# A graph network's GRU aggregations: float32 operands, or bf16 parts that sum to them exactly

## Chip, core and metric

The kernel runs on one NeuronCore of one Trainium2 chip. The metric is the device time of one execution, in microseconds (us). The time before is a median of three runs. The profile is one further execution, recorded by the hardware profiler. Engines are named as in the profile: PE is TensorE, PEld its weight loads, DVE is VectorE, ACT is ScalarE, POOL is GpSimd, and SP is the queue that issues all the DMAs.

## What is computed

128 graphs of 128 nodes with 256 features each (`x` is 128 x 128 x 256, `adj` is 128 x 128 x 128 with integer entries). Two layers, both behind a layer norm and a ReLU and both added to the input:

```
h = relu(layernorm(x));  A = (adj != 0)
for l in 0, 1, 2:                              # gated graph layer
    m = h @ weight[l]
    aggr[t] = sum over s of A[s, t] * m[s]
    h = gru_cell(aggr, h, w_ih, w_hh, b_ih, b_hh)
x = x + h
h = relu(layernorm(x))                         # graph attention layer
Wh = h @ W.T;  e[i, j] = leaky_relu(Wh[i].a1 + Wh[j].a2), -inf where adj is 0
x = x + softmax(e) @ Wh
```

## The kernel before

**Tiling.** Four graphs form a group (G = 4, T = 512 nodes); 32 groups with three GRU layers each make 96 GRU steps. A group's state is kept in two layouts: `h`, rows of nodes (128 x 4 x 256, nodes on the partitions), and `hT`, columns (128 x 2 x 512, features on the partitions). The weight of the layer is folded into the input weights beforehand, so that a step needs first the sum over neighbours of the state itself: `gathered` (L630) takes, for each of two feature chunks and four graphs, one float32 matmul with a 128 x 128 piece of `h` as the stationary operand and the graph's A as the moving one (L637). Its two PSUM banks are copied by ACT into `aT` (L663), the columns of the aggregate. The same function serves the attention layer at the end, with softmax weights (tile e or prT) in A's place.

**One GRU step** (`gru_step`, L710) is two passes of `blocks` (L749) with seven `product`s each. They are Strassen-like block products: stationary sums of weight blocks, prepared once, against halves and sums of halves of hT and aT (`moving_sums`, L484, four subtractions on DVE for each, L493). All of them go into five PSUM banks: u, m (m7), c1 twice and c2. Between the products ACT copies u and m out (L757, L760, L770), and DVE adds u and m: into c2 at L763, into the SBUF tile c22 at L774. The next product into u needs those reads of u to be done. The gates follow on ACT (L795, L802, L830) and DVE (L837), then the new state on DVE: L682, L694, L696 and L698, each 128 x 1024 with operands in SBUF.

**From columns to rows.** After a step the new hT becomes h either by PE transposes (`rows`, L618, at the two ends of the run), or, for most steps, by DVE's 32 x 32 block transposes (L590) and two sets of four DMAs that pass through DRAM (`to_rows_by_blocks`, L581).

**The prologue and epilogue of a group.** `prologue` (L905) normalises x into h and makes A out of adj with `not_equal` (L919). `epilogue` (L940) is the attention layer; `mask` (L927) turns A in place into 0 and -1e30, which is added to the scores (L1055; for the two last groups by a matmul of ident with A, L1009). POOL does only three instructions of four columns for each layer norm (`norm_scales`, L454 to L458).

**What sets the order.** The program is one long list, written out by a planner that runs while the kernel is built (`Order`, L173). Each piece of work is a generator that yields an engine, a reckoned length, the time when its data are ready, and perhaps a `room`, a buffer that has to be free. The planner keeps a clock for each engine and takes the task that can start first, by rank. A clock "port" is shared by POOL and by those DVE operations that are yielded as DVE2: the planner never lets them overlap (L186, L196). The products of a GRU step are placed in a fixed order, with other DVE and ACT work filled in between (`fill`, L264) and other PE work between products (`matmuls`, L280). What comes out is the order of instructions on each engine; on the chip each engine runs its list in order, and an instruction starts as soon as its semaphores allow.

The steps of three groups take turns: (g, 0), (g-1, 1), (g-2, 2), and so on. `settle` (L1173) adds `inputs` (L647) of the next step's group while a step is being placed: the state's sums, the aggregation, the copies to aT and their sums.

Of the kernel before, what the change touches and what calls it, by code (L numbers as in the profile page):

```python
# [7 lines left out]

F32 = mybir.dt.float32
I32 = mybir.dt.int32  # L10
AF = mybir.ActivationFunctionType
ALU = mybir.AluOpType
AX = mybir.AxisListType

P = 128
D = 256
C = D // P
G = 4
T = G * P
H = T // 2  # L20
# [7 lines left out]
def preln_gnn_kernel(  # L28
# [14 lines left out]
    nc = tc.nc  # L43
# [4 lines left out]
    io = ctx.enter_context(tc.tile_pool(name="io", bufs=6))  # L48
# [8 lines left out]
    put = on_pe  # L57
# [4 lines left out]
    XT, AT = 3, 2  # L62
# [12 lines left out]
    work = ctx.enter_context(tc.tile_pool(name="work", bufs=2))  # L75
    gate = ctx.enter_context(tc.tile_pool(name="gate", bufs=2))
    small = ctx.enter_context(tc.tile_pool(name="small", bufs=4))

    ident = const.tile([P, P], F32, name="ident")
    make_identity(nc, ident)  # L80

    def borrowed(pool, shape, tag, name, columns, **bufs):
        tile_ = pool.tile(shape, F32, tag=tag, name=name, **bufs)
        flat = tile_.rearrange("p a b -> p (a b)") if len(shape) == 3 else tile_
        return flat[:, 0:columns]
# [10 lines left out]
            cols = slice(gates.start * D, gates.stop * D)  # L98
            dma(w[k][:, cols], weight[k * P : (k + 1) * P, cols])

    def load_weight(l, pool, shape, tag):
        w = borrowed(pool, shape, tag, f"wt_{l}", C * D)
        w = w.rearrange("p (c d) -> p c d", d=D)
        dma(w, weight_t[l].rearrange("(c p) d -> p c d", p=P))
        wt.append(w)
# [29 lines left out]

    zero = borrowed(gate, [P, C, T], "r", "zero", T, bufs=1).bitcast(mybir.dt.bfloat16)[:, 0:T]
    put(nc.vector.memset(zero, 0.0))
    c1 = [ps_sum.tile([P, 2, H], F32, name=f"c1_{n}") for n in range(2)]  # L140
    c2 = ps_sum.tile([P, 2, H], F32, name="c2")
# [23 lines left out]
    PE, ACT, DVE, DVE2, POOL, SP = "PE", "ACT", "DVE", "DVE2", "POOL", "SP"  # L165
    HOP = 0.2
# [6 lines left out]
    class Order:  # L173
        def __init__(self):
            self.free = dict.fromkeys((PE, ACT, DVE, POOL, SP, "port"), 0.0)
            self.tasks = []

            self.rooms = {room: [0.0] * 2 for room in ("tq", "x1", "prT", "e", "hs")}
            self.rooms |= {"misc": [0.0] * 3, "h": [0.0] * ROWS}
            self.next, self.room_of = dict.fromkeys(self.rooms, 0), {}  # L180

# [36 lines left out]
        def open(self, room, name):  # L218
            self.room_of[name] = room, self.next[room]
            self.next[room] = (self.next[room] + 1) % len(self.rooms[room])  # L220
            if room == "misc" and self.room_of[name][1] > 2:

                return more[self.room_of[name][1] - 3].rearrange("p n t -> p (n t)")
            if room == "misc":
                return ps_misc.tile([P, T], F32, tag="misc", name=name)
            if room == "h":
                return work.tile([P, G, D], F32, tag="h", name=name, bufs=ROWS)
            if room in ("prT", "e"):
                return work.tile([P, G, P], F32, tag=room, name=name)
            if room == "x1":  # L230
                return io.tile([P, G, D], F32, tag="x1", name=name, bufs=2)
            return work.tile([P, C, T], F32, tag=room, name=name)
# [79 lines left out]
    order = Order()  # L312
# [317 lines left out]
    def gathered(h, A, ready, name, graphs=range(G)):  # L630
# [13 lines left out]
            banks.append(pa)  # L644
        return banks, t

    def inputs(s, ready):  # L647

        name = f"{s.g}_{s.l}"
        s.tH, s.tA = {}, {}  # L650
        parts = len(s.parts())
        s.hidden = order.add(0, moving_sums(s.hT, s.tH, ready, f"h_{name}", parts))
        if s.l and not s.by_blocks():
            s.h, s.h_ready = yield from rows(s, ready, name)
        banks, ready = yield from gathered(s.h, s.A, s.h_ready, f"pa_{name}")
        order.close(f"h_{name}" if s.l else f"h_a{s.g}", ready)
        aT = None
        for c, pa in enumerate(banks):
            t = yield ACT, 0.57, ready
            order.close(f"pa_{name}_{c}", t)  # L660
            if aT is None:
                aT = columns_tile("aT", name)
            put(nc.scalar.copy(aT[:, c, :], pa))  # L663
        s.aT, s.aT_ready = aT, t
        yield from moving_sums(aT, s.tA, t, f"a_{name}", parts)

    def state_rows(s):
        s.h, s.h_ready = yield from to_rows_by_blocks(s.hT, s.hT_ready, f"{s.g}_{s.l}")
# [41 lines left out]
    def gru_step(s, last, part):  # L710
# [38 lines left out]
        def blocks(no, gates):  # L749

            m = gate.tile([P, 2, H], F32, tag="m", name=f"m_{name}_{no}")
            c22 = gate.tile([P, 2, H], F32, tag="c22", name=f"c22_{name}_{no}")
            done = product(gates, lambda q: u[:, q, 0:W], W11, (0, 0), None, banks["u"], True, (ACT,))
            t = order.take(ACT, bank_t, max(done, banks["c1_0"]))
            put(nc.scalar.copy(c1[0][:, :, 0:W], u[:, :, 0:W]))  # L757
            done = product(gates, lambda q: m7[:, q, 0:W], S3, None, T3, 0.0, True, (ACT,))
            tm = order.take(ACT, bank_t, done)
            put(nc.scalar.copy(m[:, :, 0:W], m7[:, :, 0:W]))  # L760
            done = product(gates, lambda q: u[:, q, 0:W], S2, None, T2, t, False, (DVE,))
            t = order.fixed(DVE, full_t, max(done, tm, banks["c2"]))
            put(nc.vector.tensor_tensor(  # L763
                c2[:, :, 0:W], u[:, :, 0:W], m[:, :, 0:W], ALU.add
            ))
            done = product(gates, lambda q: c1[0][:, q, 0:W], W12, (1, 0), None)
            yield done
            done = product(gates, lambda q: u[:, q, 0:W], S1, None, T1, t, False, (ACT,))
            t = order.take(ACT, bank_t, max(done, banks["c1_1"]))
            put(nc.scalar.copy(c1[1][:, :, 0:W], u[:, :, 0:W]))  # L770

            order.fill(t, (DVE,))
            tc22 = banks["u"] = order.fixed(DVE, full_t, t)
            put(nc.vector.tensor_tensor(  # L774
                c22[:, :, 0:W], u[:, :, 0:W], m[:, :, 0:W], ALU.add
            ))
            done = product(gates, lambda q: c2[:, q, 0:W], N22, None, T4, 0.0, False, (ACT, DVE))
            yield c22, tc22, done
            done = product(
                gates, lambda q: c1[1][:, q, 0:W], S4, (1, 1), None, t, False, (ACT, DVE)  # L780
            )
            yield done
# [26 lines left out]
        c22, t22, done = next(phase)  # L809
# [95 lines left out]
    def prologue(s):  # L905

        g = s.g
        kept = []
        parts = s.scales if g == 0 else [s.scales]
        for i, (rstd, nb, t) in enumerate(parts):  # L910
            n = G // len(parts)
            graphs = range(i * n, i * n + n)
            s.h, t = yield from norm_apply(s.xt, graphs, rstd, nb, t, f"a{g}", kept)
        s.h_ready = t
        if g + XT < NG:
            order.add(1, load_task(load_rows, xts, g + XT, t))
        t2 = yield DVE, 0.36, s.at_ready
        s.A = work.tile([P, G, P], F32, tag="A", name=f"A_{g}", bufs=6)
        put(nc.vector.tensor_scalar(s.A, s.at, 0.0, None, ALU.not_equal))  # L919
        if g + AT < NG:  # L920
            order.add(1, load_task(load_adjacency, ats, g + AT, t2))
        transposed = to_columns if g < 2 else to_columns_by_blocks
        s.hT, s.hT_ready = yield from transposed(s.h, t, f"a{g}")
        if s.entered:
            s.task = order.add(0, inputs(s, s.hT_ready))
# [14 lines left out]
    def epilogue(s, hT, graphs, ready):  # L940
# [46 lines left out]
        place = min(part.start, G - 2)  # L987
        for i in (1, 0):
            for k in graphs:
                first = not late and s.prT is None  # L990
                t = yield (DVE2, 0.53, ready, "prT") if first else (DVE2, 0.53, ready)
                if s.prT is None and late:
                    s.prT = io.tile([P, G, P], F32, tag="at", name=f"prT_{g}", bufs=AT)
                if s.prT is None:
                    s.prT = order.open("prT", f"prT_{g}")

                unused = s.prT[:, place : place + 2, :].rearrange("p k s -> p (k s)")
                put(nc.vector.scalar_tensor_tensor(
                    unused, h[:, k, :], rstd[:, k : k + 1] if final_one else 1.0, wa[:, i, :],
                    ALU.mult, ALU.mult,  # L1000
                    accum_out=(one, two)[i][:, k : k + 1],
                ))

        if late:
            t = yield PE, 4 * graph_t if end else graph_t, max(t, s.off_ready), "misc"
            p2 = order.open("misc", f"ps2_{name}")
            if end:

                put(nc.tensor.matmul(  # L1009
                    p2[:, cols], ident, s.A[:, part, :].rearrange("p k s -> p (k s)"),  # L1010
                    start=True, stop=False, skip_group_check=True,
                ))
            for k in graphs:
# [86 lines left out]
        final = graphs[-1] + 1 == G  # L1100
        if final:
            order.close(f"h_b{g}_0", ready)
        if final and not end:
            order.close(f"e_{g}", ready)
        for c, pq in enumerate(banks):
# [184 lines left out]
```

## Time and profile before

| | us |
|---|---|
| median of three runs (lowest, highest) | 2126.3 (2125.74, 2128.18) |
| profiled execution, first to last instruction (span) | 2124.5 |
| PE busy | 2116.6 |
| PEld busy | 1886.8 |
| DVE busy | 1733.1 |
| ACT busy | 1301.4 |
| POOL busy | 126.5 |

The page gives the span for the profiled execution and no other time of it; the median of the runs is 1.8 us above the span. The granted clock of TensorE is 1.000 on the mean. Busy times overlap, each engine has its own. In the groups, a line reads: line of the kernel, engine, operation, out<-in, shapes, count, then busy time in all, mean ns of one, and the idle time of that engine just before them with what ended it. The mean ns of a matmul is its latency, not its pace, because matmuls are pipelined; the pace is read from how far apart they start. In a timeline, a row is start, length, engine, line, operation and count.

### The profile page before, as it was taken

To read this page: it belongs to the slowest core of one execution; us is meant where nothing else is said; L and a number is where in the kernel's file an instruction comes from. 1 tells how busy PE (TensorE), PEld (TensorE's weight loads), DVE (VectorE), ACT (ScalarE), POOL (GpSimd) and SP (SyncE) were. 2 spreads that over 40 slices of the span, in tenths; PEclk is the share of its full clock that TensorE was granted. 3 is DMA by queue.
4 is the path that set the end of the run, shared out by engine and by line. 5 is a ranking of instruction groups with operands and counts; after the bars stand their busy time and mean duration, and the time that the engine had idled before them with its cause. 6 is when DMAs were issued, how large, how long until landed. Compare 5 with 4: busy or idle time off the path is not lost.

```text
span 2124.5 us, 32340 instructions
## 1 busy us (share of the span) xinstructions
PE 2116.6 (100%) x10865; PEld 1886.8 (89%) x10865; DVE 1733.1 (82%) x3771; ACT 1301.4 (61%) x2875; POOL 126.5 (6%) x200
## 2 busy tenths in 40 slices
PE   9999999999999999999999999999999999999999
PEld 7888888888888888888888888888888888888888
DVE  7778888888878888888888888888888888787777
ACT  5556666566656666666656666666666566665666
POOL 1000000000000000000000000000000000000000
PEclk9999999999999999999999999999999999999999
DMA  5334454554455444545344554445453544444311
GB/s 159 65 85 88 86 118 107 107 117 92 98 115 119 84 96 107 122 109 113 83 108 104 117 122 82 98 106 123 110 107 88 107 107 105 96 98 94 70 31 46
DMA packets 667975, 211.95 MB, mean 100 GB/s; under 512 B 578336, under 2 KB 644640, under 8 KB 667808
## 3 DMA queue, kind: packets, MB, share of 16 engines
q1 hardware_dynamic: 667808, 209.87, 44.3%
q8 instruction: 86, 1.41, 0.3%
q14 instruction: 81, 0.66, 0.1%
HBM read 121.91 MB, written 87.88 MB: 99 GB/s over the span
## 4 chain that ended last, share of the span: by engine, by line
PE 98%; DVE 1%; ACT 0%; DMA 0%; issue 0%; POOL 0%; SPq 0%; ACTq 0%; DVEq 0%
PE c L737 35%; PE u L737 35%; PE m L737 12%; PE pa L637 8%; PE po L1124 5%; PE pq L637 2%; PE pw L378 0%; DMA xt<-in_x 0%; PE c L1124 0%; PE u L1124 0%; ACT v L688 0%; PE c L637 0%; PE pr_o L527 0%; DVE st_a L440 0%; PE pr L527 0%; ACT e L1065 0%
## 5 line engine op out<-in xcount | busy, mean ns | idle before, releaser
L830 ACT ACTIVATE z<-c,brz 128x256 f32<-128x256 f32 (+1 forms) x388 | 186.2, 480 | 328.4 <-PE c L737 186.4
L737 PE MATMUL u<-t_h,s_hh 128*128 128x256 f32 (+1 forms) x1164 | 345.0, 378 | 0.9 <-DVE c L763 0.5
L737 PE MATMUL u<-t_a,s_f 128*128 128x256 f32 (+1 forms) x1164 | 312.3, 377 | 0.0
L737 PE MATMUL c<-aT,s_f 128*128 128x256 f32 (+1 forms) x1164 | 312.3, 377 | 0.0
L795 ACT ACTIVATE r<-c,brz 128x256 f32<-128x256 f32 (+1 forms) x388 | 175.3, 475 | 194.3 <-PE c L737 112.8
L763 DVE TENSOR_TENSOR c<-u,m 128x512 f32<-128x512 f32 (+1 forms) x194 | 134.6, 694 | 140.8 <-PE u L737 140.4
L737 PEld LDWEIGHTS u<-t_h,s_hh 128*128 128x128 f32 x1164 | 218.4, 190 | 31.3 <-ACT c L757 1.6
L737 PEld LDWEIGHTS c<-aT,s_f 128*128 128x128 f32 x1164 | 220.4, 190 | 28.9
L737 PEld LDWEIGHTS u<-t_a,s_f 128*128 128x128 f32 x1164 | 220.4, 190 | 29.0
L737 PE MATMUL c<-hT,s_hh 128*128 128x256 f32 (+1 forms) x780 | 229.8, 376 | 0.0
L837 DVE TENSOR_TENSOR v<-v,c 128x256 f32<-128x256 f32 (+1 forms) x388 | 153.6, 415 | 66.3 <-PE c L737 43.7
L770 ACT COPY c<-u 128x512 f32<-128x512 f32 (+1 forms) x194 | 109.7, 566 | 117.5 <-PE u L737 116.1
L760 ACT COPY m<-m 128x512 f32<-128x512 f32 (+1 forms) x194 | 112.7, 581 | 107.1 <-PE m L737 106.9
L802 ACT ACTIVATE v<-c,bhn 128x256 f32<-128x256 f32 (+1 forms) x388 | 173.0, 474 | 0.0
L737 PE MATMUL m<-t_h,s_hh 128*128 128x256 f32 (+1 forms) x582 | 172.3, 378 | 0.0
L737 PE MATMUL c<-t_h,s_hh 128*128 128x256 f32 (+1 forms) x582 | 172.1, 377 | 0.0
L737 PEld LDWEIGHTS c<-hT,s_hh 128*128 128x128 f32 x780 | 147.6, 190 | 19.2
L774 DVE TENSOR_TENSOR c<-u,m 128x512 f32<-128x512 f32 (+1 forms) x194 | 131.8, 679 | 37.9 <-ACT c L770 34.9
L737 PE MATMUL u<-aT,s_f 128*128 128x256 f32 (+1 forms) x582 | 156.2, 377 | 0.0
L737 PE MATMUL m<-t_a,s_f 128*128 128x256 f32 (+1 forms) x582 | 156.1, 377 | 0.0
L737 PE MATMUL c<-t_a,s_f 128*128 128x256 f32 (+1 forms) x582 | 156.1, 377 | 0.0
L757 ACT COPY c<-u 128x512 f32<-128x512 f32 (+1 forms) x194 | 109.8, 566 | 43.7 <-PE u L737 43.7
(164 smaller groups left out, 3928.4 us busy)
## 6 DMA issues: line engine op xcount, KB each, us to landing
z<-tq SPq DMA_DIRECT2D x248, 128.0 KB
h<-z SPq DMA_DIRECT2D x248, 128.0 KB
xt<-in_x SPq DMA_DIRECT2D x31, 512.0 KB
z_a<-tq_a SPq DMA_DIRECT2D x120, 128.0 KB
hT_a<-z_a SPq DMA_DIRECT2D x120, 128.0 KB
z_b<-tq_b SPq DMA_DIRECT2D x116, 128.0 KB
h_b<-z_b SPq DMA_DIRECT2D x116, 128.0 KB
x<-in_x SPq DMA_DIRECT2D x29, 512.0 KB
```

Source lines behind the costliest of these rows:

```text
L637: put(nc.tensor.matmul(pa[:, k * P : (k + 1) * P], h[:, k, c * P : (c + 1) * P], A[:, k, :], start=True, stop=True,))
L737: put(nc.tensor.matmul(to(q), S[0][:, gate_no, weight, :], moving, start=first and q == 0 and i == 0, stop=(i == len(ends) - 1), skip_grou ...
L757: put(nc.scalar.copy(c1[0][:, :, 0:W], u[:, :, 0:W]))
L760: put(nc.scalar.copy(m[:, :, 0:W], m7[:, :, 0:W]))
L763: put(nc.vector.tensor_tensor(c2[:, :, 0:W], u[:, :, 0:W], m[:, :, 0:W], ALU.add))
L770: put(nc.scalar.copy(c1[1][:, :, 0:W], u[:, :, 0:W]))
L774: put(nc.vector.tensor_tensor(c22[:, :, 0:W], u[:, :, 0:W], m[:, :, 0:W], ALU.add))
L795: put(nc.scalar.activation(r[:, o, cols], src, AF.Tanh, bias=brz[:, o : o + 1], scale=0.5))
L802: put(nc.scalar.activation(v[:, o, cols], src, AF.Identity, bias=bhn[:, o : o + 1], scale=0.5))
L830: put(nc.scalar.activation(z[:, o, cols], src, AF.Tanh, bias=brz[:, C + o : C + o + 1], scale=0.5))
L837: put(nc.vector.tensor_tensor(v[:, o, cols], v[:, o, cols], src, ALU.add))
L1124: put(nc.tensor.matmul(po[:, j, :], hs[:, c, k * P : (k + 1) * P], gwt[:, c, :], start=(c == 0), stop=(c == C - 1),))
```

## The change

The aggregations of the GRU steps no longer multiply float32 by float32. A becomes a bf16 tile (its entries are 0 and 1). h is split into three bf16 parts which sum to it exactly: the first is the upper half of each float32 word, read where it stands; POOL subtracts it from h (the remainder goes to a new tile `rest`); the second part is the upper half of each word of that remainder; POOL subtracts it too and writes the third part, in bf16, into the lower halves of the same words. Each aggregation matmul becomes three bf16 matmuls that accumulate in PSUM. The two subtractions stand in the planner's list ahead of the aggregation. The attention layer's own aggregation stays as it was.

To go with that: the matmul of ident with A (L1009) takes a bf16 view of ident; c22 gets one buffer where it had two; the buffers for the late prT are booked with the planner in a room of their own; `load_weight` passes buffer counts on.

```diff
+    ident_b = ident.bitcast(BF16).rearrange("p (c n) -> p c n", n=2)[:, :, 1]
...
+    def by_parts(tile_):
+
+        halves = tile_.bitcast(BF16).rearrange("p g (d n) -> p g d n", n=2)
+        return halves[:, :, :, 0], halves[:, :, :, 1]
+
+    def split(h, ready, name):
+
+        _, first = by_parts(h)
+        t = yield POOL, 2.4, ready, "rest"
+        rest = order.open("rest", f"rest_{name}")
+        third, second = by_parts(rest)
+        put(nc.gpsimd.tensor_tensor(rest, h, first, ALU.subtract))
+        t = yield POOL, 2.4, t - HOP
+        put(nc.gpsimd.tensor_tensor(third, rest, second, ALU.subtract))
+        return (first, second, third), t
+
+    def gathered_by_parts(parts, A, ready, name):
+
+        banks = []
+        t = yield PE, 0.17 * C * G, ready, "misc", C
+        for c in range(C):
+            pa = order.open("misc", f"{name}_{c}")
+            for k in range(G):
+                for i, h in enumerate(parts):
+                    put(nc.tensor.matmul(
+                        pa[:, k * P : (k + 1) * P],
+                        h[:, k, c * P : (c + 1) * P],
+                        A[:, k, :],
+                        start=(i == 0),
+                        stop=(i == len(parts) - 1),
+                    ))
+            banks.append(pa)
+        return banks, t
+
     def inputs(s, ready):
...
-        banks, ready = yield from gathered(s.h, s.A, s.h_ready, f"pa_{name}")
+        parts, ready = yield from split(s.h, s.h_ready, name)
+        banks, ready = yield from gathered_by_parts(parts, s.A, ready, f"pa_{name}")
         order.close(f"h_{name}" if s.l else f"h_a{s.g}", ready)
+        order.close(f"rest_{name}", ready)
...
-            c22 = gate.tile([P, 2, H], F32, tag="c22", name=f"c22_{name}_{no}")
+            c22 = gate.tile([P, 2, H], F32, tag="c22", name=f"c22_{name}_{no}", bufs=1)
...
-        s.A = work.tile([P, G, P], F32, tag="A", name=f"A_{g}", bufs=6)
+        s.A = work.tile([P, G, P], BF16, tag="A", name=f"A_{g}", bufs=6)
...
-                    p2[:, cols], ident, s.A[:, part, :].rearrange("p k s -> p (k s)"),
+                    p2[:, cols], ident_b, s.A[:, part, :].rearrange("p k s -> p (k s)"),
...
+        if final and late:
+            order.close(f"prT_{g}", ready)
```

More of the change, by code (lines that the diff above doesn't have):

```diff
@@ L10 @@
 I32 = mybir.dt.int32
+BF16 = mybir.dt.bfloat16
 AF = mybir.ActivationFunctionType
@@ L99, in load_gates, with load_weight @@
             dma(w[k][:, cols], weight[k * P : (k + 1) * P, cols])
-    def load_weight(l, pool, shape, tag):
-        w = borrowed(pool, shape, tag, f"wt_{l}", C * D)
+    def load_weight(l, pool, shape, tag, **bufs):
+        w = borrowed(pool, shape, tag, f"wt_{l}", C * D, **bufs)
         w = w.rearrange("p (c d) -> p c d", d=D)
@@ L133, in preln_gnn_kernel @@
         xts[g] = load_rows(g), 18.0 + 2.0 * g
-    zero = borrowed(gate, [P, C, T], "r", "zero", T, bufs=1).bitcast(mybir.dt.bfloat16)[:, 0:T]
+    zero = borrowed(gate, [P, C, T], "r", "zero", T, bufs=1).bitcast(BF16)[:, 0:T]
     put(nc.vector.memset(zero, 0.0))
@@ L176, in __init__ @@
             self.tasks = []
-            self.rooms = {room: [0.0] * 2 for room in ("tq", "x1", "prT", "e", "hs")}
+            self.rooms = {room: [0.0] * 2 for room in ("tq", "x1", "prT", "e", "hs", "rest", "late")}
             self.rooms |= {"misc": [0.0] * 3, "h": [0.0] * ROWS}
@@ L227, in open @@
                 return work.tile([P, G, D], F32, tag="h", name=name, bufs=ROWS)
+            if room == "late":
+                return io.tile([P, G, P], F32, tag="at", name=name, bufs=AT)
+            if room == "rest":
+                return work.tile([P, G, D], F32, tag="rest", name=name)
             if room in ("prT", "e"):
@@ L650, in inputs @@
         s.tH, s.tA = {}, {}
-        parts = len(s.parts())
-        s.hidden = order.add(0, moving_sums(s.hT, s.tH, ready, f"h_{name}", parts))
+        n_parts = len(s.parts())
+        s.hidden = order.add(0, moving_sums(s.hT, s.tH, ready, f"h_{name}", n_parts))
         if s.l and not s.by_blocks():
             s.h, s.h_ready = yield from rows(s, ready, name)
-        banks, ready = yield from gathered(s.h, s.A, s.h_ready, f"pa_{name}")
+        parts, ready = yield from split(s.h, s.h_ready, name)
+        banks, ready = yield from gathered_by_parts(parts, s.A, ready, f"pa_{name}")
         order.close(f"h_{name}" if s.l else f"h_a{s.g}", ready)
+        order.close(f"rest_{name}", ready)
         aT = None
@@ L664, in inputs @@
         s.aT, s.aT_ready = aT, t
-        yield from moving_sums(aT, s.tA, t, f"a_{name}", parts)
+        yield from moving_sums(aT, s.tA, t, f"a_{name}", n_parts)
     def state_rows(s):
@@ L989, in epilogue @@
             for k in graphs:
[L990 to L993, printed above, removed]
+                room = "late" if late else "prT"
+                t = yield (DVE2, 0.53, ready, room) if s.prT is None else (DVE2, 0.53, ready)
                 if s.prT is None:
-                    s.prT = order.open("prT", f"prT_{g}")
+                    s.prT = order.open(room, f"prT_{g}")
                 unused = s.prT[:, place : place + 2, :].rearrange("p k s -> p (k s)")
```

## The prediction

> **What bounds the kernel now.** I read the page's busy times first, then its chain, and then asked which engine is idle and how close the others follow.
>
> ```profile
> PE 2116.6 (100%) x10865; PEld 1886.8 (89%) x10865; DVE 1733.1 (82%) x3771; ACT 1301.4 (61%) x2875; POOL 126.5 (6%) x200
> ...
> PE 98%; DVE 1%; ACT 0%; DMA 0%; issue 0%; POOL 0%; SPq 0%; ACTq 0%; DVEq 0%
> PE c L737 35%; PE u L737 35%; PE m L737 12%; PE pa L637 8%; PE po L1124 5%; PE pq L637 2%; PE pw L378 0%; DMA xt<-in_x 0%; PE c L1124 0%; PE u L1124 0%; ACT v L688 0%; PE c L637 0%; PE pr_o L527 0%; DVE st_a L440 0%; PE pr L527 0%; ACT e L1065 0%
> ```
>
> TensorE (PE) is the bound: it carries 98% of the chain, and every nanosecond taken from its stream comes off the span, as long as nobody is late for it. The aggregations (pa, L637) are 8% of the chain. The second thing to see is VectorE (DVE) at 82%: it is not on the chain, but it is the engine that must never be late. The groups by form, then a timeline of 4 us in mid-run, show what it does and with how little room:
>
> ```profile
> L763 DVE TENSOR_TENSOR c<-u,m 128x512 f32<-128x512 f32 x190 | 132.9, 699 | 138.3 <-PE u L737 137.9
> ...
> L637 PE MATMUL pa<-A,h 128*128 128x128 f32 x1024 | 124.7, 275 | 0.0
> ...
> L637 PE MATMUL pa<-A,h_a 128*128 128x128 f32 x512 | 62.4, 275 | 0.0
> ```
>
> ```profile
> 1003.41 0.70 DVE L763 TENSOR_TENSOR c<-u,m 128x512 f32<-128x512 f32 x1 [0.49 <-PE u L737]
> ...
> 1004.23 0.41 PEld L737 LDWEIGHTS u<-t_h,s_hh 128*128 128x128 f32 x2
> ...
> 1004.44 0.59 PE L737 MATMUL u<-t_h,s_hh 128*128 128x256 f32 x2
> ```
>
> L763 reads bank u; the next matmul into u waits for it. It ends at 1004.11 and that matmul starts at 1004.44: 0.33 us of slack. In front of it DVE sat idle for 0.73 us on the mean (the page's 140.8 us over 194). So, twice in each GRU step, a DVE that is more than about 0.73 + 0.33 = 1.06 us behind stops TensorE.
>
> **Part 1, the matmuls: 96 aggregations change.** A float32 matmul leaves two passes in the trace: 1024 + 512 = 1536 passes over 96 aggregations is 16 each, for 8 matmuls. The timeline has such a set as x16 in 1.95 us; less the last one's 0.275 that is 1.675/15 = 0.112 us a pass, 16 x 0.112 = 1.79 us. After the change there are 24 bf16 passes. What is one worth? The trace has three bf16 matmuls, in the first microseconds:
>
> ```profile
> 1.17 1.46 PE L146 MATMUL c<-zero 128*128 128x512 bf16 x3 [1.17 <-DVE zero L139]
> ...
> 9.18 0.19 PEld L378 LDWEIGHTS pw<-wih,wt 128*128 128x128 f32 x1 [0.24 <-issue]
> ...
> 9.61 0.19 PEld L378 LDWEIGHTS pw<-wih,wt 128*128 128x128 f32 x1 [0.24 <-ACT h_a L471]
> ```
>
> Each of the three lasted about 0.635 (the median of that line), so they start (1.46 - 0.635)/2 = 0.41 us apart for 512 columns. In the same early stage float32 passes of 256 columns follow each other in 0.43 us (the loads at 9.18 and 9.61), against 0.216 later in the run. So a bf16 column costs half of a column of a float32 pass, and 128 of them 0.112/2 = 0.056 us. The weight load could bind instead. A float32 load of 128 columns paces its matmuls at about 0.10 to 0.11 us even when they stream only 2 columns (L409: eight pairs, first starts 50.4 to 51.1). A bf16 load was recorded at 105, 117 and 152 ns (L146), the float32 one at 190: 38 to 85 ns less, so a pace of 0.025 to 0.07 us. But those weights lay side by side; the new ones sit in every second 16-bit word, which no row shows. Bounds for the pass: 0.056 to 0.112 us. I take 0.056, since the bf16 rows are the nearer ones. **Gain: 96 x (1.79 - 24 x 0.056) = 96 x 0.446 = 42.8 us**; with 0.112 instead it is a loss of 96 x (2.69 - 1.79) = 86 us.
>
> The page "TensorE: Matmul & The Clock Gate" of the Trainium skill, section "Back-to-back issue gap", speaks against this: it gives about 81 ns for a sustained load-and-matmul pair at 128 columns. By that figure the sum below would have, as an estimate, a loss of 96 x (24 x 0.081 - 1.79) = 15 us where I have the gain of 42.8. No row here shows such a stream in bf16.
>
> The two end groups' matmul with ident (L1009, float32: 0.93 us for 512 columns, two halves of 0.43) goes to a quarter: about -1.3 us, at the very end.
>
> **Part 2, two GpSimd (POOL) instructions for each aggregation, 192 in all.** Each subtracts over 128x1024. POOL has no such row. Lower bound: DVE's own two-input operation of this size, 1.22 us (L694). Nearest POOL row: the 128x128 select of the identity took 0.293 us (masks.py:199), one input; eight times that is 2.3. The code reckons 2.4. I take 2.3 and keep 1.2 to 3. As work on POOL this is 192 x 2.3 = 442 us in an engine idle for 94% of the time, and in mid-run the transfers that bring the state's rows (h<-z on SP) are issued some 20 us ahead of their aggregation (the last at 769.4, the aggregation at 789.5), so TensorE should not wait for the parts themselves. Only at the start there is no such lead: h_a is done at 11.58, the first aggregation starts at 12.62 and its result is first used at 16.64. Two subtractions put it at about 16.4, and its use some 3 us later: **+3 us**.
>
> **What the POOL work meets is DVE.** The timeline around a small POOL chain shows it:
>
> ```profile
> 791.54 1.23 DVE L694 TENSOR_TENSOR hT<-hT,v 128x1024 f32<-128x1024 f32 x1 [0.37 <-ACT v L688]
> ...
> 792.27 0.59 POOL L456 TENSOR_SCALAR norm_b<-mv_b 128x4 f32<-128x4 f32 x1
> ...
> 792.80 1.23 DVE L696 SCALAR_TENSOR_TENSOR hT<-z,hT 128x1024 f32<-128x1024 f32 x1
> 792.94 1.15 POOL L458 TENSOR_TENSOR norm_b<-norm_b 128x4 f32<-128x4 f32 x1
> ```
>
> L458 works on 4 elements and takes 0.22 us elsewhere (its norm_a rows); here it takes 1.15 and ends 0.06 us after L696, a DVE operation with two inputs in SBUF. L456 likewise ends just after L694. So the two engines exclude each other for such operations; that a long POOL operation stops DVE in turn is my inference, since the trace has no long one. The page "SBUF — State Buffer" of the Trainium skill, section "Who interferes with whom", says so outright: whoever starts first holds the port for the whole instruction, and the other stands. If that rule held only in the direction that the rows show, the sum below would lose its stall term and end at 2085.
>
> How much does DVE lose? In 65 us (three GRU steps; window 765 to 830) its operations with two SBUF inputs (L493, L682, L694, L696, L698, L971, L998, L1055) take 30.5 us by their groups, the others 23.5, and 11.0 are idle. POOL gets six of the 2.3 us operations in there. During 2.3 us DVE has on the mean 30.5/65 x 2.3 = 1.1 us of work that cannot run; since its queue is in order, the first such operation holds up everything behind it, up to the full 2.3. Half of these operations follow one another without a gap, so I take 1.3: 6 x 1.3 = 7.8 us of delay per 65 us. Bounds: 0 (order perfect) to 6 x 2.3 = 13.8.
>
> What of that reaches TensorE? L763 comes six times in the 65 us, and each can swallow 1.06 us. Spread evenly, 1.3 on each, 0.24 x 6 = 1.4 us get through, or 1.4 x 32 = 46 us over the run. But the two subtractions are issued as a pair, and where both delays fall before the same L763, 2.6 us meet 1.06 and (2.6 - 1.06) x 3 x 32 = 148 us get through. The list that places instructions does know that DVE and POOL exclude each other and will move DVE's work around. Yet POOL's instruction waits only for its data, which are early, so it starts before the time that the list gave it and meets other DVE work. I take the middle: **+97 us** of waits of TensorE for DVE.
>
> The other edits cost nothing that I can find. c22 with one buffer: L774 writes it every 9 us or so, its readers (L795, L802, L830, L837) are done within about 4; were that cover gone, L774 would wait up to 0.5 us. A in bf16: L919, L930 and L1055 (0.42, 0.42, 0.69 us, 30-odd times) stay or shrink. The bookkeeping of the late prT buffer issues nothing new. A, written by DVE once a group, keeps its queue position, and SP's queue is not touched.
>
> **Sum**: 2124.5 (span) - 42.8 - 1.3 + 3 + 97 = 2180.4. The median of the runs shown is 2126.3, 1.8 above the profiled span; the page has no other time for that execution. So 2182.
>
> **Rivals.**
> - *Faster: the list's new order keeps two-input DVE work out of POOL's way.* One mechanism, at L763: it decides when the delay that passes the 1.06 us is under 41.1/192 = 0.21 us per subtraction. DVE's 11 us of idle in 65 exceed my 7.8 of delay, which speaks for it; POOL's early start speaks against. Stalls of 0 to 37 us give 2085 to 2122; at 10, 2095. Chance 0.33.
> - *The weight loads of strided bf16 run at float32 pace* (0.112 us): 2182 + 42.8 + 86 = 2311 with the stalls, 2214 without. Then the change doesn't do what it says, three passes are simply more than two. Chance 0.08.
> - *Gain and stall cancel*, within 0.2% (4.3 us, about what a measurement of this kernel can tell from no change): 0.05.
> - Forecast, stalls above the gain: 0.54, from 2131 to 2250.
>
> Faster 0.33, same 0.05, slower 0.62. Range: the low end is the rival with no stall, 2085, less 2 for a pass of 0.055; the high end is the lumped stall, 2182 + 51 = 2233, plus 17 for a subtraction of 2.5 us and more. That is 2083 to 2250; what is left out are the slow loads with stalls and a subtraction near 3 us. The likeliest case alone spans 2131 to 2250.
>
> **What would show it.** Aggregations: 24 passes in about 1.5 us, starts 56 ns apart (112: the loads bind). POOL near 570 us busy, subtractions of 2.3 us (more where they stand behind DVE). DVE: idle time before L493, L682, L694 to L698 or L998 put down to POOL; if there is none, my inference on the exclusion is wrong. PE: idle before u (L737) put down to DVE L763 or L774, in sum about 97 us, and PE's share of the chain below 95%. A wait of PE pa for POOL of more than a few us would mean that the parts come too late, which I have not priced.

## The result, and the profile after

| | before | after |
|---|---|---|
| median of the runs, us | 2126.3 | 2455.2 (2451.9 to 2459.4) |
| ratio to before, 95% interval | | 1.1545 (1.1529 to 1.1562) |
| span of the profiled execution, us | 2124.5 | 2453.0 |
| mean granted clock of PE | 1.000 | 0.948 |

The change costs 329 us. The prediction had the sign, with 2182, but the time lies 205 us above the top of its range. The page of after, its busy times, the clock in 40 slices, and the chain:

```profile
PE 2169.8 (88%) x11629; PEld 1880.9 (77%) x11630; DVE 1924.3 (78%) x3771; ACT 1304.8 (53%) x2875; POOL 510.9 (21%) x392
...
PEclk9999998999989989998999899989989998999998
...
PE 71%; DVE 20%; ACT 3%; issue 2%; DMA 2%; SPq 2%; POOL 0%; DVEq 0%; ACTq 0%
```

PE is now idle for 283 us of its span (2453.0 - 2169.8); before it was 8. DVE carries 20% of the chain where it had 1%. DVE issues the same 3771 instructions as before, but they are busy for 191 us longer. And the clock, which was 1.000, dips at regular places. The waits show whom PE waits for (columns: us in total, times, longest):

```profile
PE pq L643 <- DMA e<-z_e: 102.7, 8, 14.2
...
PE u L779 <- ACT c L799: 66.7, 10, 16.6
...
PE u L779 <- DVE c L805: 63.0, 24, 5.8
...
PE u L779 <- DVE c L816: 27.3, 18, 2.2
```

Two kinds stand out. The DVE rows are what the prediction had in mind: 63.0 + 27.3 = 90.3 us, many and short. The upper two are something else: eight waits of some 13 us in which the attention layer's scores product (pq, the old L637) waits for a DMA of softmax weights, and ten, of 6.7 us on the mean and 16.6 at most, before a product into u. Before, the first of these rows is absent and the second comes to 0.4 us, and in mid-run the change leaves the attention layer's work as it was.

The changed work itself is quick. Three rows in mid-run and a group by form:

```profile
1067.73 0.22 PE L677 MATMUL pa<-A,h 128*128 128x128 bf16 x1
...
1067.79 0.28 PE L677 MATMUL pa<-A,rest 128*128 128x128 bf16 x2
...
1067.90 0.22 PE L677 MATMUL pa<-A,h 128*128 128x128 bf16 x1
```

From the first of these passes to the fourth it is 0.17 us (1067.73 to 1067.90); over all aggregations a pass starts 56 ns after the one before it, in the median. The subtractions took 1.96 us in the median (1.89 to 2.87).

### The profile page after: what moved, and what is told of

It is laid out like the page before. It is cut to its first block, busy times and chain, and to the rows that moved or that the text cites. A ratio compares the mean times of both kernels' runs of the same rounds, so it can differ in the third digit from the quotient of the medians.

```text
span 2453.0 us, 34120 instructions
## 1 busy us (share of the span) xinstructions
PE 2169.8 (88%) x11629; PEld 1880.9 (77%) x11630; DVE 1924.3 (78%) x3771; ACT 1304.8 (53%) x2875; POOL 510.9 (21%) x392
## 4 chain that ended last, share of the span: by engine, by line
PE 71%; DVE 20%; ACT 3%; issue 2%; DMA 2%; SPq 2%; POOL 0%; DVEq 0%; ACTq 0%
PE u L779 27%; PE c L779 25%; PE m L779 8%; PE pa L677 4%; PE po L1166 4%; DVE prT L1038 3%; DVE t_a L499 3%; DVE hT L736 2%; DVE hT L738 2%; DVE hT L740 2%; SPq L61 2%; PE pq L643 1%; DVE c L805 1%; DVE t_h L499 1%; DMA e<-line 1%
## 5 line engine op out<-in xcount | busy, mean ns | idle before, releaser
L779 PE MATMUL u<-t_h,s_hh 128*128 128x256 f32 (+1 forms) x1164 | 366.1, 397 | 130.2 <-ACT c L799 66.7
L779 PE MATMUL u<-t_a,s_f 128*128 128x256 f32 (+1 forms) x1164 | 325.2, 390 | 0.0
L805 DVE TENSOR_TENSOR c<-u,m 128x512 f32<-128x512 f32 (+1 forms) x194 | 134.2, 692 | 155.9 <-PE u L779 135.1
L779 PEld LDWEIGHTS u<-t_a,s_f 128*128 128x128 f32 x1164 | 227.9, 197 | 32.8
L664 POOL TENSOR_TENSOR rest<-h 128x1024 f32<-128x1024 f32 x64 | 126.5, 1976 | 569.8 <-DMA h<-z 443.1
L812 ACT COPY c<-u 128x512 f32<-128x512 f32 (+1 forms) x194 | 109.7, 566 | 215.2 <-PE u L779 213.9
L460 POOL TENSOR_TENSOR norm_a<-norm_a,mhalf 128x4 f32<-128x4 f32 (+1 forms) x33 | 34.5, 1046 | 901.4 <-DVE norm_a L452 674.0
L666 POOL TENSOR_TENSOR rest<-rest 128x1024 bf16<-128x1024 f32 x96 | 209.3, 2181 | 7.5
L879 DVE TENSOR_TENSOR v<-v,c 128x256 f32<-128x256 f32 (+1 forms) x388 | 164.9, 447 | 56.8 <-PE c L779 44.0
L724 DVE SCALAR_TENSOR_TENSOR v<-r,v 128x1024 f32<-128x1024 f32 (+1 forms) x97 | 142.9, 1473 | 46.4 <-ACT v L844 45.7
L816 DVE TENSOR_TENSOR c<-u,m 128x512 f32<-128x512 f32 (+1 forms) x194 | 132.1, 681 | 55.6 <-ACT c L812 54.2
L779 PE MATMUL c<-t_a,s_f 128*128 128x256 f32 (+1 forms) x582 | 161.6, 388 | 0.0
```

The source lines that it names most:

```text
L664: put(nc.gpsimd.tensor_tensor(rest, h, first, ALU.subtract))
L666: put(nc.gpsimd.tensor_tensor(third, rest, second, ALU.subtract))
L724: put(nc.vector.scalar_tensor_tensor(v_, flat(r, cols), 1.0, v_, ALU.add, ALU.mult))
L779: put(nc.tensor.matmul(to(q), S[0][:, gate_no, weight, :], moving, start=first and q == 0 and i == 0, stop=(i == len(ends) - 1), skip_grou ...
L805: put(nc.vector.tensor_tensor(c2[:, :, 0:W], u[:, :, 0:W], m[:, :, 0:W], ALU.add))
L816: put(nc.vector.tensor_tensor(c22[:, :, 0:W], u[:, :, 0:W], m[:, :, 0:W], ALU.add))
```

## Experiments

A measure that I use below: for each matmul, the time from its start to the next one's, less the median of that interval for its kind. Summed over the run this is the time that PE lost to waits and to a lowered clock ("lost" from here on). The sum of the medians is its paced work. (A kind is a line of the kernel with its shapes.) Before: 2112.0 paced, 7.9 lost. After: 2067.4 and 380.9. So the matmul stream got 44.6 us shorter, and 373 us of loss came in. Theories for that loss: **LOCK** (the expectations call it PORT), a POOL subtraction stops DVE's two-input operations, and the late DVE stops PE; **ORDER**, the planner, which has to keep 4.8 us of the shared port free for each aggregation, writes a worse list; **EARLY**, POOL runs ahead of its place in the list, so that it meets DVE work which the list had kept clear of it.

**The matmuls alone** (`e1_no_remainders`)

```diff
-        parts, ready = yield from split(s.h, s.h_ready, name)
+        parts, ready = 3 * (by_parts(s.h)[1],), s.h_ready
```

> No POOL subtractions and none in the planner's list: the first bf16 part is multiplied three times, so the remainders are left out of the sum, and the 24 bf16 passes stay. Both theories: the matmuls alone, 2126 - 43 = about 2085, between 2075 and 2100. Above 2126 the loss would lie in the bf16 passes themselves, which neither theory holds.

Measured: 2096.9, ratio 0.986 (0.9845 to 0.9875), clock 0.999. Paced work is 2068.6, as in after. The net gain is 29.4 and not 43, because 21.5 us are lost instead of 7.9; the biggest piece is one wait of 5 us near the end of the run, which before does not have. The cause of the 373 us is thus not in the matmuls.

**The order alone** (`e2_plan_only`): everything is booked as in after, but the two POOL instructions are not issued. DVE's and ACT's instructions stand in the same order in both traces.

```diff
-        rest = order.open("rest", f"rest_{name}")
-        third, second = by_parts(rest)
-        put(nc.gpsimd.tensor_tensor(rest, h, first, ALU.subtract))
+        order.room_of[f"rest_{name}"] = "rest", order.next["rest"]
+        order.next["rest"] = (order.next["rest"] + 1) % 2
         t = yield POOL, 2.4, t - HOP
-        put(nc.gpsimd.tensor_tensor(third, rest, second, ALU.subtract))
-        return (first, second, third), t
+        return (first, first, first), t
```

> The order of all instructions as in the changed kernel (the planner still books 2 x 2.4 us of POOL and of the shared port for each aggregation), but the two subtractions are not issued; the first part is multiplied three times, so the remainders are left out. Theory PORT (long POOL instructions stop DVE, and TensorE waits for DVE): near the run without any remainders, 2085 to 2130. Theory ORDER (the planner, made short of port time, writes an order in which every third group's attention layer comes late and TensorE has to wait for its transfers): the loss stays, 2330 to 2455.

Measured: 2319.0, ratio 1.0908 (1.089 to 1.0926), clock 0.958. That is 222 us above e1, with no subtraction on POOL at all, and 11 us below what was expected of ORDER. Its page and its waits:

```profile
PE 2123.3 (92%) x11630; PEld 1867.4 (81%) x11630; DVE 1726.8 (75%) x3771; ACT 1310.8 (57%) x2875; POOL 109.1 (5%) x200
```

```profile
PE pq L643 <- DMA e<-z_e: 102.6, 8, 14.6
...
PE u L777 <- ACT c L797: 65.2, 10, 17.3
```

The long waits of after are all here (102.6 of 102.7 us, 65.2 of 66.7), while the DVE rows are nearly gone (1.6 us for L803, 0.9 for L814). So the long waits are ORDER, and the short ones for DVE are not. A timeline shows how such a wait is made:

```profile
616.52 1.03 PE L777 MATMUL c<-aT,s_f 128*128 128x256 f32 x4
...
617.58 0.42 DVE L877 TENSOR_TENSOR v<-v,c 128x256 f32<-128x256 f32 x1 [0.35 <-PE c L777]
...
617.92 0.70 DVE L616 STREAM_TRANSPOSE prT<-e 128x512 f32<-128x512 f32 x1
...
621.80 1.29 SPq L61 DMA_DIRECT2D z_e<-prT  x2
...
628.20 1.70 SPq L61 DMA_DIRECT2D e<-z_e  x4
...
631.63 3.75 PE L643 MATMUL pq<-e,h_b 128*128 128x128 f32 x16 [14.09 <-DMA e<-z_e]
```

Read it backwards. pq is next in PE's list; it needs e, which comes back from DRAM by the DMAs of 628.20; these need z_e; that needs DVE's transposition L616 at 617.92; and L616 stands in DVE's list behind L877, which waits for the product at 616.52 that PE has only just done. Nothing in this row of work can start before PE is through, and pq stands next in PE's list. Before, the same L610 runs at 778.16 and pq at 792.57, with the DMAs between them under PE's other work.

The long wait before u follows some 20 us later and is the same lump one step on. In after, for the pq wait at 897.6, the chain reads:

```profile
922.47 1.65 ACT e L1105 x8
924.11 0.95 ACT hs L1158 x2
925.06 0.49 ACT c L799
...
925.60 2.93 PE u L779 x6
```

L799 is the copy that frees bank u, and in ACT's list the next softmax (L1105, L1158) stands ahead of it, whose scores had come back by DMA only at 919.57.

The list is why. Before, the port carries, by the prediction's count, 30.5 us of DVE work in 65 us. Booking 3 x 4.8 = 14.4 more leaves 20 of 65, and the attention layer's tasks, which have the last rank (2), are put off until they are forced out in a lump, every third group: the long wait for pq comes at 667, 898, 1127 and 1354 us of after, 229 us apart. The planner's own clock, which the list is written by, ends at 2132 for before and at 2343 for after: the list as written already has the waits in it.

**The subtractions alone** (`e3_unbooked`): the whole change, but the planner reckons the two POOL instructions on a clock of their own, not on the port.

```diff
+    POOL2 = "Q7"
...
-            self.free = dict.fromkeys((PE, ACT, DVE, POOL, SP, "port"), 0.0)
+            self.free = dict.fromkeys((PE, ACT, DVE, POOL, POOL2, SP, "port"), 0.0)
...
-        t = yield POOL, 2.4, ready, "rest"
+        t = yield POOL2, 2.4, ready, "rest"
...
-        t = yield POOL, 2.4, t - HOP
+        t = yield POOL2, 2.4, t - HOP
```

> The whole change with both subtractions on POOL, but the planner books them on a clock of their own and not on the port that POOL and DVE share, so DVE's order stays close to the one without them. Theory PORT: POOL stops DVE at least as much as in the changed kernel, 2300 to 2460. Theory ORDER: 2085 plus some waits of TensorE for a DVE that POOL stops, 2090 to 2200.

Measured: 2252.5, ratio 1.059 (1.0574 to 1.0605), clock 0.984. This lies between the two expectations. A planner that ignores the exclusion is 203 us faster than one that respects it. The long waits are gone, although the bookings keep their length and their buffers: it was the port that made them. What is left is PE waiting for DVE:

```profile
PE u L780 <- DVE c L806: 90.9, 54, 3.5
...
PE u L780 <- DVE c L817: 5.8, 4, 3.3
```

LOCK by itself costs 155.6 us here (e3 - e1), and 136.2 in after's list (after - e2). The second is the cleaner number, since after and e2 have one list; those of e3 and e1 differ a little (their planner's clocks end at 2103 and 2098). How the port stops DVE is seen in a timeline of after:

```profile
1002.23 2.56 POOL L664 TENSOR_TENSOR rest<-h 128x1024 f32<-128x1024 f32 x1 [5.21 <-DMA h<-z]
...
1003.83 3.28 DVE L499 TENSOR_TENSOR t_a<-aT 128x256 f32<-128x256 f32 x2
...
1004.87 1.96 POOL L666 TENSOR_TENSOR rest<-rest 128x1024 bf16<-128x1024 f32 x1
...
1006.79 2.07 POOL L664 TENSOR_TENSOR rest<-h_a 128x1024 f32<-128x1024 f32 x1
1007.14 2.00 DVE L499 TENSOR_TENSOR t_a<-aT,t_a 128x256 f32<-128x256 f32 x1
...
1008.94 1.96 POOL L666 TENSOR_TENSOR rest<-rest 128x1024 bf16<-128x1024 f32 x1
1009.17 2.00 DVE L499 TENSOR_TENSOR t_a<-t_a,aT 128x256 f32<-128x256 f32 x1
```

Four subtractions of two aggregations stand back to back for 8.7 us. In that time DVE gets four operations of 0.42 us through, one in each change of hands: 1.7 us of work in the 7.3 from 1003.83 to 1011.17. Note that such a stop is not an idle time in the records but a longer operation: L499 takes 2.00 instead of 0.42. Counted over the run (an operation is stretched when it lasts over 0.1 us more than the quick ones of its kind), before, e1 and e2 have none, after has 155, by 209 us in all, and e3 158 by 195. That is 209/155 = 1.35 us a stop. The Trainium skill's page "SBUF — State Buffer", section "Who interferes with whom", has the rule that the prediction leaned on: the engine that comes first keeps the shared port for its whole instruction. This trace agrees: L499 at 1007.14 comes after the subtraction of 1006.79 and ends at 1009.14, 0.28 us behind it.

**A shorter booking** (`e4_len16`): after with `yield POOL, 1.6` in both places.

> The whole change, with each subtraction booked at 1.6 us on the port instead of 2.4. Theory PORT: the instructions on POOL are the same, so the time stays near the changed kernel's, 2380 to 2460. Theory ORDER: the shorter booking leaves the port enough room for the attention layer's work, 2100 to 2200.

Measured: 2251.3, ratio 1.058 (1.0558 to 1.0602). The time lies below what was expected of LOCK and above what was expected of ORDER. The list recovers (its own clock ends at 2108), but the stops are nearly all there again: 151 operations stretched, by 176 us. This shorter booking mends the list and protects next to nothing.

**The attention layer ranked earlier** (`e8_rank`, and `e5_rank_len20`, where the booking is also 2.0): the rank is what decides who is put off.

```diff
-            order.add((1.8 if s.g >= NG - 2 else 1.9 if s.g == NG - 3 else 2), epilogue(s, new, graphs, t))
+            order.add((1.8 if s.g >= NG - 2 else 1.9 if s.g == NG - 3 else 0.4), epilogue(s, new, graphs, t))
```

> The changed kernel with one number changed: the attention layer's tasks have rank 0.4 instead of 2, the booking stays 2 x 2.4 us. The planner's clock for PE ends at 2174 instead of 2343. Theory ORDER (the booked port starves the low rank, the attention layer then stands in PE's way): about 170 of the 222 us that the order alone cost go, 2260 to 2330. If the order's loss were not a matter of the attention layer being put off: 2420 to 2460.

> The whole change, each subtraction booked at 2.0 us (what POOL took for it in the changed kernel's trace is 1.96), and the attention layer's tasks given rank 0.9 instead of 2, so that they are no longer put off. The planner's own clock for PE then ends at 2120 (2343 for the changed kernel, 2132 for the kernel before, which took 2126). If the chip kept to the order's own times: 2110 to 2130. Theory EARLY (POOL starts as soon as its data are there, ahead of its place in the planner's time, and so stops DVE work that the planner had kept clear of it): 2180 to 2270, as without any booking.

Measured: e8 2267.9, ratio 1.0669 (1.0653 to 1.0685); e5, with 0.9 for the 0.4, 2220.9, ratio 1.0443 (1.0428 to 1.0459). One number in e8, with every booking as in after, takes back 187 us (after - e8), and the long waits shrink, for pq from 102.7 us and before u from 66.7, to this:

```profile
PE u L779 <- ACT c L799: 28.8, 11, 8.6
...
PE pq L643 <- DMA e<-z_e: 1.6, 2, 0.9
```

So most of the 222 us of ORDER is the attention layer being put off. How the 187 split between ORDER and LOCK is not measured, since e8's list was not run without its subtractions. With that mended, 136 (e5) to 148 (e8) operations are still stretched, though the list keeps the port clear.

**POOL held to its place** (`e6_held`): as e5, but DVE writes one column of `rest` first, at the place that the list gave the subtraction, so that POOL can't start earlier. The diff is against after; the second length and the rank are as in e5. This asks whether EARLY is why a list that keeps clear of the port still meets it.

```diff
-        t = yield POOL, 2.4, ready, "rest"
+        t = yield DVE, 0.06, ready, "rest"
         rest = order.open("rest", f"rest_{name}")
         third, second = by_parts(rest)
+        put(nc.vector.memset(rest[:, 0, 0:1], 0.0))
+        t = yield POOL, 2.0, t
...
```

> As the run before with rank 0.9 and 2.0 us, but each pair of subtractions is held back to its place: DVE first writes one column of the tile rest, which the first subtraction overwrites, so POOL waits for DVE to come to that point. The planner's clock ends at 2118. Theory EARLY: POOL now runs where the planner put it, so most of the stall goes: 2110 to 2150. If it is POOL's occupancy alone that costs, wherever it lies: no better than the run without the hold, 2180 to 2270.

Measured: 2214.5, ratio 1.0407 (1.0382 to 1.0432). That is 6.4 us below e5 and hardly clear of the spread of the runs (2205.0 to 2218.0, and 2217.8 to 2223.5 in e5); the 2110 to 2150 that were expected of EARLY were not reached. As to the stops EARLY is right in part: they fall from 171 to 97 us. As to the time it hardly matters, since another wait grows in their place:

```profile
PE pa L679 <- POOL rest L668: 30.4, 14, 2.6
...
PE u L781 <- DVE c L807: 15.9, 9, 5.1
...
PE pa L679 <- POOL rest L666: 14.9, 12, 1.9
```

The waits for DVE go down to 15.9 from e5's 38.0, and the aggregation now waits for POOL for 45.3 us (30.4 + 14.9) where it was 34.3. Running early was a harm to DVE and a cover for PE at once.

**One subtraction, and two kept apart** (`e7_one_unbooked`, `e9_apart`), both made from e3. In e7 the second subtraction and its booking are left out; in e9 a DVE copy of one column of `rest`, placed 5 us after the first, stands ahead of the second. The diff is e9's, against after:

```diff
...
-        t = yield POOL, 2.4, t - HOP
+        t = yield DVE, 0.08, t + 5.0
+        put(nc.vector.tensor_copy(rest[:, 0, 0:1], rest[:, 0, 0:1]))
+        t = yield POOL2, 2.4, t
```

> As the run with the subtractions on a clock of their own, but only the first subtraction of each pair is issued; the third part is replaced by the first, so the second remainder is left out and the 24 passes stay. None of the pair: 2097; both: 2252. Theory PORT in proportion: half the stall, 2097 + 78 = about 2175, 2150 to 2190. If only the pair in a row is what stops TensorE (a single block is swallowed by DVE's idle time): 2100 to 2130.

> The whole change, subtractions on a clock of their own as before (2252 with the pair in a row; 2134 with only one of the two issued; 2097 with none), but the second subtraction is kept apart from the first: DVE copies one column of rest onto itself, placed 5 us after the first, and the second waits for that. If it is the pair in a row that beats TensorE's slack (a single stop of DVE is mostly swallowed by its idle time): 2097 + 2 x 37 = about 2170, 2150 to 2200. If the cost goes by POOL's occupancy alone: 2252 stays, 2235 to 2270.

Measured: e7 2133.6, ratio 1.0035 (1.0021 to 1.0049); e9 2189.0, ratio 1.0292 (1.0275 to 1.031). Above e1, one subtraction costs 36.7 us, a pair back to back 155.6, a pair kept apart 92.1. e7 lies just above the range for a single block that DVE's idle time swallows, and e9 within the range for a pair kept apart. The stops come to 78 us in e7, 195 in e3 and 208 in e9. So e9 has no less of them than e3, differently spaced, and takes 63 us less, although its aggregation waits 17.3 us for the second subtraction and the copy (11.1 and 6.2). The lists of the three aren't the same, but their planner's clocks lie close (2103, 2103 and 2106). The main wait in e9:

```profile
PE u L782 <- DVE c L808: 21.8, 37, 0.9
```

In e3 this wait is 54 times up to 3.5 us; in e9 it is 37 times up to 0.9. So a single stop mostly fits into DVE's slack of about 1 us, two in a row don't. (Part of the 63 us is the clock, of which below: its mean is 0.984 in e3 and 0.997 in e9.)

**A version in two parts** (`e10_two_parts`): one subtraction, booked 2.0; the attention layer ranked 1.2.

```diff
-        t = yield POOL, 2.4, ready, "rest"
+        t = yield POOL, 2.0, ready, "rest"
...
-        t = yield POOL, 2.4, t - HOP
-        put(nc.gpsimd.tensor_tensor(third, rest, second, ALU.subtract))
-        return (first, second, third), t
+        return (first, second), t
...
-        t = yield PE, 0.17 * C * G, ready, "misc", C
+        t = yield PE, 0.113 * C * G, ready, "misc", C
...
```

> Two bf16 parts instead of three and one subtraction instead of two, booked at 2.0 us; the attention layer's tasks have rank 1.2; 16 bf16 passes for an aggregation, booked at 0.113 for two. The third part is left out, so the parts sum to h's upper 16 significant bits or so, not to all of h. Passes: 96 x 8 x 0.056 = 43 us less than with three parts, so 2097 - 43 = 2054 without stalls (the planner's clock for PE ends at 2070); a single subtraction cost 37. Both theories: 2085 to 2115, below both kernels. If DVE stops cost as much as with a pair: 2150 or more.

Measured: 2075.1, ratio 0.9758 (0.9744 to 0.9773). Two thirds of the passes, half of POOL's work, and a list that doesn't put the attention layer off beat both kernels by 51 us or more, and come in 10 us under the expected range; 43.4 us are lost, on top of 2026.5 paced. The price is exactness, since the third part is left out of the sum. A version with all three parts below 2126 was not found.

## Why the prediction was wrong, step by step

**PE bounds, DVE must not be more than about 1.06 us late.** Right. The waits of e9, at most 0.9 us each, and of e3, up to 3.5, are in keeping with that bound.

**The matmuls, 42.8 us, with 0.056 us a pass.** Right: 56 ns, and 44.6 us less paced work (L1009 included). Weights in every second 16-bit word load fast enough, and the rival of slow loads fell. The 81 ns that the page "TensorE: Matmul & The Clock Gate" of the Trainium skill gives under "Back-to-back issue gap" did not show here, and the measured 56 decide. Of the gain 29.4 us reach the end in e1.

**POOL, 2.3 us an instruction, and +3 us at the start.** Near: 1.96 in the median. At the start the first aggregation waits 1.46 us for POOL and its sums' product 2.7 more.

**POOL's long operation stops DVE.** The inference was right (155 operations, none before). The count of what it stops left out the operations on A (L961, L972), which have one input in SBUF and are stopped too.

**Stops of 1.3 us, of which 97 us reach PE: a term that was mis-sized.** A stop is 1.35 us, and the text's two cases, spread evenly (46) and in a pair (148), have runs that come near them: 92 with the pair kept apart, 155.6 (e3) or 136.2 (after) as it is. The subtractions do come as a pair, and the middle had no row to stand on; the lumped case should have been taken. The waits put down to DVE come to 96.7 us in e3 (90.9 + 5.8) and 90.3 in after, which only looks like a hit: of the rest of the 155.6, some 40 us are losses of under 0.5 us each (47.0 in e3, 7.1 in e1), mostly slow passes after the waits (see the last section).

**"The list that places instructions does know that DVE and POOL exclude each other and will move DVE's work around": this step failed.** I let it only help, as the mechanism of the rival "faster", and priced what moving costs at nothing. It cost 222 us (e2 - e1), more than the exclusion that it is there to avoid, and the exclusion's 136.2 us came on top all the same. A sign was at hand: the planner's own clock ends at 2343 for after and at 2132 for before, 211 us apart, and it is known when the kernel is built. The port's numbers, 14.4 us more where 30.5 of 65 were taken, point the same way but don't give the size (see Open). The result is made up of these differences between runs, which add up to it by their making:

2126.3 - 29.4 (matmuls, e1) + 222.1 (order, e2) + 136.2 (stops, after - e2) = 2455.2.

**"It starts before the time that the list gave it."** True: held to its place (e6), POOL stops DVE for 97 us instead of 171. It is worth 6 us at most by itself, because the early start also covers the aggregation's wait for POOL.

**The other edits at nothing.** No row speaks against it: c22's wait for its readers doesn't appear. `mask` on A in bf16 (L972) takes 0.28 us in the median instead of 0.42.

**The signs.** PE's chain share fell below 95% (71), POOL's busy time is 511 of 570, DVE's stops appear as longer operations and not as idle time put down to POOL, as I had written; by that sign I would have called a right inference wrong.

**Open.** Why the list tips over just where it does: bookings of 1.6 and 1.8 give planner's clocks of 2108 and 2121, 1.9 gives 2358, and after's 2.4 gives 2343, so that the clock does not simply grow with the booking. I followed its result, not its single choices.

## What to carry to other kernels

When a written order reserves a shared resource, price the reservation as well as the contention: run the order without the work, and the work without the reservation, and look at the planner's own clock before either. Two short stops that mostly fit into an engine's slack one at a time can cost four times one of them when they come back to back (36.7 us for one, 92.1 for two apart, 155.6 for two in a row). And a lock shows as longer operations, not as idle time: compare the duration of a kind with itself before the change.

## What the runs showed of the hardware that was not expected

**The clock after a wait.** Four windows around one long wait of after (columns: the window, its length, busy time of each engine, granted clock, DMA share, GB/s):

```profile
870.00:897.50 27.50, 27.50 (x147) 24.28 (x146) 23.87 (x47) 18.79 (x44) 0.41 (x1) 1.00 0.30 68
897.50:915.00 17.50, 3.60 (x18) 3.23 (x17) 12.72 (x38) 4.25 (x8) 2.62 (x6) 0.63 0.78 138
915.00:930.00 15.00, 7.77 (x27) 6.27 (x27) 4.54 (x10) 4.87 (x16) 0.00 (x0) 0.75 0.18 36
930.00:950.00 20.00, 20.00 (x120) 17.89 (x119) 8.04 (x16) 7.67 (x16) 8.40 (x4) 1.00 0.51 145
```

PE waits 14 us there, from 897.6 on, and the granted clock is 0.63 and 0.75 on the mean until it is back at 1.00. Cut finer, it is 0.50 in two stretches and 1.00 between them; no other value is on record in this run:

```profile
902.20:915.80 13.60, 3.92 (x17) 3.91 (x18) 8.51 (x30) 2.08 (x4) 1.48 (x3) 0.50 0.68 130
915.80:922.60 6.80, 2.57 (x12) 1.90 (x10) 1.38 (x2) 1.41 (x5) 0.00 (x0) 1.00 0.13 39
922.70:929.40 6.70, 3.80 (x9) 3.08 (x10) 3.16 (x8) 3.36 (x12) 0.00 (x0) 0.50 0.25 39
```

The passes behind such a wait are slow: the sixteen of pq at 631.63 in e2 take 3.75 us, where fifteen of them took 1.84 before (at 792.57). Losses of 0.06 to 0.5 us at a pass come to 89.1 us over after (528 of them), 47.0 over e3, and 7.1 over e1. About 80 of after's 89 us lie within 6 us of a wait of over 0.5 us, and 68 of the 89, as 31 of e3's 47, lie in stretches at 0.5; what lies outside them is not slow passes. In e9 it is 4 of 56: there nearly all waits are short, and the mean clock is 0.997. So a long wait of PE is paid for again in the passes behind it, and the prediction had no such term.

**Which operations the port stops.** POOL's subtractions are stopped by DVE as well (1.89 us alone, up to 2.99 in e3). Of DVE's operations, L961 (L962 in e3), which turns adj into A with one input in SBUF, is stretched too, by 27.9 us over its 32 in e3. In e9 the 128x4 operation of the second layer norm on DVE (L453, norm_b), one input too, takes 0.52 us on the mean where it takes 0.17 before. The 32 x 32 transpositions, the layer norm's statistics (0.40 us before and after) and the sums out of PSUM (L805, L816) are not stretched, though many of them start while a subtraction runs.
